# Three-term bfloat16 feed-forward with ternary weights in a four-layer gated block

## Chip, cores and metric

The kernel runs on one core of one Trainium2 chip. The metric is the device time of one execution in microseconds (us), as the median of several runs. Profile times come from one further execution under the hardware profiler, and count from the start of its span.

## What is computed

The reference is a stack of four layers, each a cross attention and a feed-forward. Both work on the layer-normalised activations `x` (4 x 256 tokens of 256 features, float32) and are added back through a gate `tanh(g)`. The layers differ in their attention and in their feed-forward: layer 0 a mixture of 16 experts, layer 1 a feed-forward with ternary weights, layer 2 a matmul quantised to 8 bits, layer 3 a mixture of 8 experts. Here layer 1's feed-forward is changed:

```python
def absmean_quant(w):
    scale = jnp.mean(jnp.abs(w))
    mask = (jnp.abs(w) >= scale * 0.7).astype(w.dtype)
    return jnp.sign(w) * mask                       # -1, 0 or 1
w1_q, w2_q = absmean_quant(w1), absmean_quant(w2)   # 1024 x 256, 256 x 1024
h = gelu(x @ w1_q.T + b1)                           # 1024 tokens x 1024
out = h @ w2_q.T + b2                               # 1024 tokens x 256
```

## The kernel before

`x` stays in on-chip memory (SBUF) for the whole kernel as eight tiles of 128 tokens by 256 features. Most work goes by two groups `g` of 512 tokens (`NG` = 2, four tiles each)[...]. The eight steps (attention and feed-forward of each layer) are written one after the other. The program is written as a dataflow on tiles: a scheduler sets the order of instructions on each engine ahead of the run and adds the waits on semaphores, so each engine runs its own fixed list. A tile of a pool tag has as many buffers as the tag's `bufs`: `mm` in PSUM has four banks, `t4` in SBUF six buffers of 1024 float32 columns, `xn` six, `xT` two.

Names that matter here:

- `big` is one large SBUF tensor of 24,576 float32 columns. It holds layer 0's attention weights and experts first. Then its second part serves as `latents()` (from column 16,384 on, the hidden values of attention 1 and of layer 1's feed-forward), and at last it holds layer 3's eight experts, 3,072 columns each.
- `load_experts3` (L297) issues two DMAs for each expert of layer 3 on the SP queue. Experts 0 to 4 are loaded at the end of `ffn0`, experts 5 to 7 after `ffn1`, when `hidden` has been read. SP's queue is in order; the loads of the shared expert (`L3_sgu`, `L3_sd`) stand in it too.
- `ternary1` (L1425) is a generator whose steps are spread over layer 0's expert loop. It makes the ternary weights of layer 1 in place on VectorE (L1451, L1452), as float32.
- `ffn1` (L1455) is the step that is changed. `normalised` makes the layernorm on VectorE (L372), transposes it on TensorE (L384) and evacuates PSUM to `xT` by ScalarE and VectorE in turn (L129, L131). `up` does 8 x 2 matmuls of 128 x 128 weights by 512 tokens for a group (L399, in the helper `mm2`), and ScalarE writes `gelu` to `hidden` (L1468). `down` does 8 matmuls for each 128 tokens, with `hidden` as the stationary side and 256 columns of `w2` moving (L1475). VectorE adds the bias into `y` (L1479) and then adds to `x` (L434). `in_turn` orders this as up of group 0, up of group 1, down of group 0, down of group 1.

Lines that the text names in other stages: L656 and L664 are products and sums of attention 0's rotary embedding on VectorE and on POOL (GpSimd), L406, L407 and L415 the steps of a softmax on VectorE, ScalarE and POOL, L838 and L1047 two 16-bit matmuls, L1490 and L1491 roundings of layer 2's quantisation on VectorE.

Of the kernel before, what the change touches and what calls it, by code (L numbers as in the profile page):

```python
# [34 lines left out]
ALU = mybir.AluOpType  # L35
# [35 lines left out]
BIG = E3 * W3  # L71
X0W = E0 * W0
HALF = 16384
NOWHERE = 16384.0
C_SLOTS = 3

# [2 lines left out]
def tile_flamingo(ctx: ExitStack, tc: tile.TileContext, a: dict, out: bass.AP):  # L79
# [7 lines left out]
    def ps_mm():  # L87
        return psum.tile([P, 512], F32, tag="mm", name="mm", bufs=4)
# [299 lines left out]
    def normalised():  # L388

        out = []  # L390
        for g in range(NG):
            xn = layernorm(g)
            out.append((transposed(xn), xn))
        return out

    def mm2(ps, w, xT):

        for c in range(2):
            nc.tensor.matmul(ps, w(c), xT[:, c, :], start=(c == 0), stop=(c == 1))  # L399
# [180 lines left out]
    def latents():  # L580
        t = big[:, HALF:].rearrange("p (g r t) -> p g r t", g=NG, r=NP)
        return [t[:, g] for g in range(NG)]
# [678 lines left out]
    def ffn0(gate):  # L1261
        normal = normalised()
        xT = [xt for xt, _ in normal]
        xd = stored([xn for _, xn in normal], "xd0")
        work, places = big[:, X0W : BIG - 400], Carver(big[:, BIG - 400 :])
        cut = Carver(work)
        route: list = []

        def routing():
            cw, mask = yield from chosen(xT, gate0, E0, K0, gate0_b, gate, 2, cut)  # L1270
            route.append(cw)
            route.append((yield from placed(cw, mask, E0, K0, NB0, W0, cut, places)))

        steps = routing()
        next(steps)
        s13 = loaded["L0_s13"][:, : 2 * W0U].rearrange("p (j c n) -> p j c n", j=2, c=2)
        s2 = loaded["L0_s2"][:FC0, :1024].rearrange("p (j f o) -> p j f o", j=2, f=2)
        held: dict = {}

        def up(t):  # L1280
            g, i = divmod(t, TPG)
            ps = ps_wide()
            for j in range(2):
                nc.tensor.matmul(
                    ps[:, j, : 2 * F0], shared_is[:, j : j + 1].to_broadcast([96, P]), bias_0, start=True, stop=False
                )
            for c in range(2):
                for j in range(2):
                    nc.tensor.matmul(
                        ps[:, j, : 2 * F0], xT[g][:, c, i * P : (i + 1) * P], s13[:, j, c, :], start=False, stop=(c == 1)  # L1290
                    )
            st = t4([P, 1024], "shared")
            s = st[:, : 2 * F0].rearrange("p (j f) -> p j f", j=2)
            nc.scalar.activation(s, ps[:, :, :F0], AF.Silu)
            nc.vector.tensor_tensor(s, ps[:, :, F0 : 2 * F0], s, ALU.mult)
            held[t] = st
            next(steps, None)

        def turn(t):
            ps = ps_mm()  # L1300
            for j in range(4):
                nc.tensor.transpose(ps[:FC0, j * P : (j + 1) * P], held[t][:, j * FC0 : (j + 1) * FC0], ident)
            nc.scalar.copy(held[t][:FC0, 512:], ps[:FC0])
            next(steps, None)

        def down(t):
            hT = held.pop(t)[:FC0, 512:]
            ps = ps_mm()
            for j in range(4):
                nc.tensor.matmul(  # L1310
                    ps[:, :D], hT[:, j * P : (j + 1) * P], s2[:, j // 2, j % 2, :], start=(j == 0), stop=(j == 3)
                )
            gated_add(t, ps[:, :D], gate)

        in_three(NT, up, turn, down)
        for _ in steps:
            pass
        used("L0_s13")
        used("L0_s2")
        cw, placing = route  # L1320
        expert = placing[2]
        choice = places([96, NB0], BF16)
        nc.vector.tensor_scalar(choice, expert[:96], expert_of, None, ALU.is_equal)

        def hTs(st, b):
            return st[:FC0, 432:688]

        diags = work[:, : PEK * NT * P].rearrange("p (k t c) -> p k t c", k=PEK, t=NT)
        fold = fold1()
        ended = []  # L1330
        ternary = ternary1()

        def between(i):
            if i % 4 == 3 and not ended:
                try:
                    next(fold)
                except StopIteration as end:
                    ended.append(end.value)
            if i > 40 and ended:
                next(ternary, None)  # L1340
            if 8 <= i < 8 + PEK * NT:
                k, t = divmod(i - 8, NT)
                nc.vector.tensor_scalar(diags[:, k, t, :], ident, placing[4][:, k, t : t + 1], None, ALU.mult)

        moe = Experts(placing, xd, K0, NB0, W0, F0, FC0, "z0", big[:, : E0 * W0], (bias_0, choice), hTs, between)
        moe.run()
        kept["fold1"] = ended[0]
        for t in range(NT):

            def bias(ps):  # L1350
                pt = ps_mm()
                nc.tensor.transpose(pt[:X0, :P], cw[:, t, :], ident)
                cwT = sb.tile([P, D], F32, tag="xn", name="cwT", bufs=6)[:X0, :P]
                nc.scalar.copy(cwT, pt[:X0, :P])
                nc.tensor.matmul(ps, cwT, b2_0, start=True, stop=False)
                return True

            done = moe.combine(t, 3, {k: diags[:, k, t, :] for k in range(PEK)}, bias)
        load_experts3(0, 5, done)
        for _ in ternary:  # L1360
            pass

# [59 lines left out]
            moe.combine(t, K3, {})  # L1422

    def ternary1():  # L1425

        n = D * 1024
        sums = small([P, 2], "sums", 1)
        for k in range(2):
            part = small([P, 16], "part", 2)  # L1430
            for i in range(4):
                nc.vector.tensor_reduce(
                    part[:, i * 4 : (i + 1) * 4],
                    loaded[f"L1_w{k + 1}"][:, i * 512 : (i + 1) * 512].rearrange("p (a b) -> p a b", a=4),
                    AX.X,
                    ALU.add,
                    apply_absolute_value=True,
                )
                yield
            nc.vector.tensor_reduce(sums[:, k : k + 1], part, AX.X, ALU.add)  # L1440
        ps = ps_mm()
        nc.tensor.matmul(ps[:, :2], ones, sums, start=True, stop=True)
        thr = small([P, 2], "thr", 1)
        nthr = small([P, 2], "nthr", 1)
        nc.vector.tensor_scalar(thr, ps[:, :2], 1.0 / n, 0.7, ALU.mult, ALU.mult)
        nc.vector.tensor_scalar(nthr, thr, -1.0, None, ALU.mult)
        for k in range(2):
            for i in range(4):
                v = loaded[f"L1_w{k + 1}"][:, i * 512 : (i + 1) * 512]
                low = sb.tile([P, 512], F32, tag="low", name="low", bufs=1)  # L1450
                nc.vector.tensor_scalar(low, v, nthr[:, k : k + 1], None, ALU.is_le)  # L1451
                nc.vector.scalar_tensor_tensor(v, v, thr[:, k : k + 1], low, ALU.is_ge, ALU.subtract)  # L1452
                yield

    def ffn1(gate):  # L1455
        b2_1 = output_bias("b2_1", a["L1_b2"].partition_broadcast(P))
        quant = [loaded["L1_w1"], loaded["L1_w2"]]
        w1 = quant[0].rearrange("p (c f) -> p c f", c=2)
        w2 = quant[1].rearrange("p (f o) -> p f o", f=8)
        xT = [x for x, _ in normalised()]  # L1460
        hidden = latents()

        def up(g):
            h = hidden[g]
            for f in range(8):
                ps = ps_mm()
                mm2(ps, lambda c: w1[:, c, f * P : (f + 1) * P], xT[g])
                nc.scalar.activation(h[:, f, :], ps, AF.Gelu, bias=b1_1[:, f : f + 1])  # L1468
            return h

        def down(g, h):
            for i in range(TPG):
                ps = ps_mm()
                for f in range(8):
                    nc.tensor.matmul(  # L1475
                        ps[:, :D], h[:, f, i * P : (i + 1) * P], w2[:, f, :], start=(f == 0), stop=(f == 7)
                    )
                y = sb.tile([P, D], F32, tag="xn", name="y", bufs=6)
                nc.vector.tensor_tensor(y, ps[:, :D], b2_1, ALU.add)  # L1479
                gated_add(g * TPG + i, y, gate)  # L1480

        in_turn(NG, up, down)
        used("L1_w1")
        used("L1_w2")
        load_experts3(5, E3)

    def quantised(q, v, inv):
# [177 lines left out]
```

## Time and profile before

| what | value |
|---|---|
| median of 3 runs | 1029.69 us (1029.3 to 1032.34) |
| the profiled execution | 1034.87 us, its span 1033.2 us |
| TensorE (PE) busy | 922.9 us, 89% |
| VectorE (DVE) busy | 511.2 us, 49% |
| ScalarE (ACT) busy | 276.0 us, 27% |
| GpSimd (POOL) busy | 308.9 us, 30% |
| mean granted TensorE clock | 0.948 |

The step `ffn1` lies between 603.9 and 666.0 us. Busy times are sums over the whole span. A float32 matmul is two records in the profile, each with a weight load (PEld) of its own. The end of a matmul is modelled, so its duration has a fixed part, and the distance between starts is the better measure of a stream. Engines work side by side. What one of them costs is read from the stage and from the chain of waits, not from its share.

### The profile page before, as it was taken

The numbers are of one execution on the slowest core, as the hardware profiler recorded it, in microseconds if no ns is written. First come the engines' busy times: TensorE is split into PE (matmuls) and PEld (weight loads), VectorE is DVE, ScalarE is ACT, GpSimd is POOL, SyncE is SP. The second block draws the span as 40 slices with busy tenths as digits, with TensorE's granted clock in tenths as the row PEclk, the third lists the DMA queues.
The fourth block names the chain that finished last, engine by engine and source line by source line (L and its number), as shares of the span: only waits on it lengthen the run. The fifth ranks groups of instructions, "written<-read, shape, count | busy, mean of one in ns | idle before, by whom it ended". The sixth has DMA issues, their size and how long they took to land.

```text
span 1033.2 us, 12983 instructions
## 1 busy us (share of the span) xinstructions
PE 922.9 (89%) x4527; PEld 604.8 (59%) x4527; DVE 511.2 (49%) x1202; ACT 276.0 (27%) x544; POOL 308.9 (30%) x298
## 2 busy tenths in 40 slices
PE   3999998999799999998899989979658899999993
PEld 3544435876668876675547855745334556566661
DVE  6535446757833334453627720568676772212223
ACT  2111113442123233232123433035204431222220
POOL 4345442210256666572002210014002302233311
PEclk9999999999989999998999999989668999999997
DMA  9200118000234333532850000510000001111103
GB/s 325 82 15 0 31 46 280 21 29 3 75 115 166 115 112 124 158 77 90 272 194 1 1 1 25 185 45 1 21 0 1 22 21 30 35 47 41 32 16 123
DMA packets 36350, 76.99 MB, mean 75 GB/s; under 512 B 5434, under 2 KB 22640, under 8 KB 34975
## 3 DMA queue, kind: packets, MB, share of 16 engines
q1 hardware_dynamic: 27551, 55.88, 16.0%
q0 software_dynamic: 8736, 20.28, 6.7%
q8 instruction: 39, 0.64, 0.3%
q14 instruction: 24, 0.20, 0.1%
HBM read 64.59 MB, written 14.42 MB: 76 GB/s over the span
## 4 chain that ended last, share of the span: by engine, by line
PE 59%; DVE 16%; issue 13%; DMA 4%; POOL 4%; ACT 3%; SPq 0%; POOLq 0%; DVEq 0%; ACTq 0%
PE wide L399 8%; PE wide L1151 6%; PE mm L1186 5%; PE mm L630 4%; PE mm L399 4%; PE mm L1475 3%; PE wide L1385 2%; PE mm L429 2%; PE wide L1162 2%; POOL zz L1198 2%; PE mm L1177 2%; PE mm L890 1%; PE mm L691 1%; PE mm L384 1%; PE mm L1134 1%
## 5 line engine op out<-in xcount | busy, mean ns | idle before, releaser
L415 POOL TENSOR_TENSOR attn<-attn,sm 128x1024 f32<-128x1024 f32 x32 | 60.8, 1901 | 227.1 <-DVE sm L414 156.9
L1171 DVE TENSOR_TENSOR blk<-wide,blk 128x176 f32<-128x176 f32 (+1 forms) x86 | 37.3, 434 | 169.3 <-ACT blk L1170 169.3
L656 DVE TENSOR_TENSOR rope<-wide,big 128x512 f32<-128x512 f32 x96 | 59.6, 682 | 65.3 <-PE wide L399 65.3
L1151 PE MATMUL wide<-big,blk 128*128 x252 | 87.3, 469 | 0.3 <-issue 0.3
L399 PE MATMUL wide<-xT,big 128*128 128x512 f32 x192 | 87.3, 601 | 0.0
L1122 POOL DMA_INDIRECT xs<-xd,big x63 | 62.6, 993 | 79.1 <-PE mm L1177 36.6
L1162 PE MATMUL wide<-big,blk 128*128 x184 | 83.0, 593 | 0.5 <-DVE blk L1136 0.5
L1198 POOL DMA_INDIRECT zz<-ring,big x63 | 64.5, 1024 | 33.8 <-DVE ring L1195 14.0
L1170 ACT ACTIVATE blk<-wide 128x176 f32<-128x176 f32 (+1 forms) x86 | 33.7, 392 | 143.7 <-PE wide L1151 71.4
L1186 PE MATMUL mm<-big,blk 88*128 x252 | 65.0, 379 | 0.5 <-ACT blk L1179 0.5
L399 PEld LDWEIGHTS wide<-xT,big 128*128 128x128 f32 x192 | 35.0, 190 | 48.1 <-issue 38.3
L630 PE MATMUL mm<-vo,attnT 128*128 128x256 f32 x256 | 61.1, 393 | 0.9 <-ACT attnT L430 0.9
L1186 PEld LDWEIGHTS mm<-big,blk 88*128 88x128 f32 x252 | 47.5, 189 | 17.7 <-ACT blk L1179 1.4
L1151 PEld LDWEIGHTS wide<-big,blk 128*128 128x128 f32 x252 | 46.3, 194 | 16.0 <-issue 2.3
L630 PEld LDWEIGHTS mm<-vo,attnT 128*128 128x128 f32 x256 | 49.1, 197 | 9.7 <-ACT attnT L430 3.3
L430 ACT COPY attnT<-mm 128x512 f32<-128x512 f32 x64 | 35.0, 588 | 67.8 <-PE mm L429 67.8
L1162 PEld LDWEIGHTS wide<-big,blk 128*128 128x128 f32 x184 | 33.1, 190 | 33.2 <-issue 32.5
L1136 DVE COPY blk<-mm 128x256 f32<-128x256 f32 x86 | 36.0, 419 | 31.8 <-PE mm L1134 31.8
L1122 POOL DMA_INDIRECT xs<-xd,scratch x23 | 22.2, 966 | 92.5 <-PE mm L1134 71.3
L384 PE MATMUL mm<-ident,xn 128*128 128x128 f32 x128 | 26.1, 346 | 25.6 <-DVE xn L372 13.0
L429 PE MATMUL mm<-ident,attn 128*128 128x128 f32 x256 | 37.6, 295 | 11.8 <-POOL attn L415 11.8
L413 DVE TENSOR_REDUCE sm<-attn 128x16 f32<-128x1024 f32 x32 | 38.9, 1214 | 14.6 <-ACT attn L407 12.5
(346 smaller groups left out, 1690.0 us busy)
## 6 DMA issues: line engine op xcount, KB each, us to landing
big<-in_L_w_gate_up SPq DMA_DIRECT2D x8, 1024.0 KB, 10.1
zt<-zz SPq DMA_DIRECT2D x16, 384.0 KB, 4.7
big<-in_L_w SPq DMA_DIRECT2D x4, 1408.0 KB, 6.8
big<-in_L_w_down SPq DMA_DIRECT2D x8, 512.0 KB, 8.7
w_L_qk<-in_L_qk SPq DMA_DIRECT2D x4, 896.0 KB, 15.2
big<-in_L_w SPq DMA_DIRECT2D x4, 704.0 KB
big<-in_L_wo SPq DMA_DIRECT2D x1, 2048.0 KB, 19.7
xd<-xn SPq DMA_DIRECT2D x16, 128.0 KB, 1.8
```

The costliest lines, as they stand in the source:

```text
L399: nc.tensor.matmul(ps, w(c), xT[:, c, :], start=(c == 0), stop=(c == 1))
L413: nc.vector.tensor_reduce(sm, e, AX.X, ALU.add)
L415: nc.gpsimd.tensor_tensor(e, e, sm.unsqueeze(2).to_broadcast([P, groups, n]), ALU.mult)
L429: nc.tensor.transpose(ps[:, i * P : (i + 1) * P], ev[:, pr * P : (pr + 1) * P], ident)
L630: nc.tensor.matmul(ps[:, :D], aT[:, s, :], vo[:, s, :], start=(s == 0), stop=(s == NP - 1))
L656: nc.vector.tensor_tensor(m[:, s, :].rearrange("q (b t) -> q b t", t=S), ps[:, s, :].rearrange("q (b t) -> q b t", t=S), table, ALU.mult,)
L1122: nc.gpsimd.indirect_dma_start(out=xs, out_offset=None, in_=self.xd, in_offset=bass.IndirectOffsetOnAxis(ap=self.gather[:, b : b + 1].bitc ...
L1151: nc.tensor.matmul(ps[:, 0, : 2 * n], st[:, c * P : (c + 1) * P], self.w[:, bass.ds(r + c * 2 * n, 2 * n)], start=False, stop=(c == 1),)
L1162: nc.tensor.matmul(ps[:, k, :n], st[:, c * P : (c + 1) * P], self.w[:, bass.ds(r + (2 * c + k) * n, n)], start=(c == 0), stop=(c == 1),)
L1171: nc.vector.tensor_tensor(s, lin, s, ALU.mult)
L1186: nc.tensor.matmul(ps[:, :D], hT[:, j * P : (j + 1) * P], self.w[: self.chunk, bass.ds(r + j * D, D)], start=(j == 0), stop=(j == self.n - 1),
L1198: s = nc.gpsimd.indirect_dma_start(out=self.z, out_offset=bass.IndirectOffsetOnAxis(ap=self.scatter[:, b : b + 1].bitcast(U32), axis=0), i ...
```

## The change

The activations of layer 1's feed-forward are split into three bfloat16 terms: the value rounded to bfloat16, the rounded rest, and the rounded rest of that. Each term is multiplied by the ternary weights, which bfloat16 holds exactly, and the three products are summed in PSUM. So a float32 matmul becomes three bfloat16 matmuls, each with a weight load.

- `ternary1` writes its result as bfloat16 into the first half of the weights' own buffer.
- `inputs(g)` takes the place of `normalised`: for each half of the features ScalarE copies PSUM to the first term, VectorE subtracts it from PSUM, ScalarE copies the rest to the second term, and VectorE subtracts that into the third. The third terms lie in a `t4` buffer, `more`.
- `up` writes `gelu` for two `f` (1024 columns) into a `t4` buffer `h`. `three_terms` splits it: ScalarE copies the first term, POOL subtracts it from `h` in place, VectorE copies the second term, and VectorE subtracts to the third. The terms of all `f` lie in `big` from column 12,288 on (`HIDDEN`), which is the place of experts 4 to 7.
- `down` uses three terms for each `f`, 24 matmuls for each 128 tokens.
- Experts 0 to 3 of layer 3 are now loaded at the end of `ffn0`, and experts 4 to 7 after `ffn1`.

```diff
+EARLY3 = 4
+HIDDEN = EARLY3 * W3
...
-        load_experts3(0, 5, done)
+        load_experts3(0, EARLY3, done)
...
+    def ternary(k):
+        return loaded[f"L1_w{k}"][:, :1024].bitcast(BF16)
+
+    def three_terms(terms, v, rest):
+        nc.scalar.copy(terms[0], v)
+        nc.gpsimd.tensor_tensor(rest, v, terms[0], ALU.subtract)
+        nc.vector.tensor_copy(terms[1], rest)
+        nc.vector.tensor_tensor(terms[2], rest, terms[1], ALU.subtract)
...
-                nc.vector.scalar_tensor_tensor(v, v, thr[:, k : k + 1], low, ALU.is_ge, ALU.subtract)
+                nc.vector.scalar_tensor_tensor(
+                    ternary(k + 1)[:, i * 512 : (i + 1) * 512], v, thr[:, k : k + 1], low, ALU.is_ge, ALU.subtract
+                )
...
-        quant = [loaded["L1_w1"], loaded["L1_w2"]]
-        w1 = quant[0].rearrange("p (c f) -> p c f", c=2)
-        w2 = quant[1].rearrange("p (f o) -> p f o", f=8)
-        xT = [x for x, _ in normalised()]
-        hidden = latents()
+        w1 = ternary(1).rearrange("p (c f) -> p c f", c=2)
+        w2 = ternary(2).rearrange("p (f o) -> p f o", f=8)
+        hidden = big[:, HIDDEN:].bitcast(BF16).rearrange("p (g k f t) -> p g k f t", g=NG, k=3, f=8)
+
+        def inputs(g):
+            two = sb.tile([P, 2, 2, TH], BF16, tag="xT", name="xT", bufs=2)
+            more = t4([P, 1024], "more")
+            third = more[:, :512].bitcast(BF16).rearrange("p (c t) -> p c t", c=2)
+            xn = layernorm(g)
+            for c in range(2):
+                ps = ps_mm()
+                for i, n in enumerate(xn):
+                    nc.tensor.transpose(ps[:, i * P : (i + 1) * P], n[:, c * P : (c + 1) * P], ident)
+                rest = more[:, 512:]
+                nc.scalar.copy(two[:, 0, c, :], ps)
+                nc.vector.tensor_tensor(rest, ps, two[:, 0, c, :], ALU.subtract)
+                nc.scalar.copy(two[:, 1, c, :], rest)
+                nc.vector.tensor_tensor(third[:, c, :], rest, two[:, 1, c, :], ALU.subtract)
+            return two[:, 0], two[:, 1], third
+
+        xT = [inputs(g) for g in range(NG)]
 
         def up(g):
-            h = hidden[g]
-            for f in range(8):
-                ps = ps_mm()
-                mm2(ps, lambda c: w1[:, c, f * P : (f + 1) * P], xT[g])
-                nc.scalar.activation(h[:, f, :], ps, AF.Gelu, bias=b1_1[:, f : f + 1])
-            return h
-
-        def down(g, h):
+            for f2 in range(4):
+                h = t4([P, 2, TH], "h")
+                for j in range(2):
+                    f = 2 * f2 + j
+                    ps = ps_mm()
+                    for k, term in enumerate(xT[g]):
+                        for c in range(2):
+                            nc.tensor.matmul(
+                                ps,
+                                w1[:, c, f * P : (f + 1) * P],
+                                term[:, c, :],
+                                start=(k == 0 and c == 0),
+                                stop=(k == 2 and c == 1),
+                            )
+                    nc.scalar.activation(h[:, j, :], ps, AF.Gelu, bias=b1_1[:, f : f + 1])
+                three_terms([hidden[:, g, k, 2 * f2 : 2 * f2 + 2, :] for k in range(3)], h, h)
+            return hidden[:, g]
+
+        def down(g, terms):
             for i in range(TPG):
                 ps = ps_mm()
                 for f in range(8):
-                    nc.tensor.matmul(
-                        ps[:, :D], h[:, f, i * P : (i + 1) * P], w2[:, f, :], start=(f == 0), stop=(f == 7)
-                    )
+                    for k in range(3):
+                        nc.tensor.matmul(
+                            ps[:, :D],
+                            terms[:, k, f, i * P : (i + 1) * P],
+                            w2[:, f, :],
+                            start=(f == 0 and k == 0),
+                            stop=(f == 7 and k == 2),
+                        )
...
-        load_experts3(5, E3)
+        load_experts3(EARLY3, E3)
```

## Prediction, made before the changed kernel was run

> **What bounds the kernel now.** I read the page's busy table first: TensorE 922.9 of 1033.2 us. That is an average, so I went to the stage that is edited, by the chain of waits (columns: start, length, what):
>
> ```profile
> 604.23 0.45 PE mm L384 x4
> ...
> 608.98 1.27 PE mm L384 x6
> 610.25 27.68 PE mm L399 x62
> 637.93 27.64 PE mm L1475 x128
> 665.57 0.02 issue
> 665.59 0.42 DVE y L1479
> ```
>
> From the first transpose (604.2) to the last `y` (666.01) TensorE sets the time: 27.7 us up, 27.6 us down, nothing between. The busy time by stretch and the groups of the stage show how idle the others are (stretch: engine busy us, records; then group: busy, mean ns, idle before):
>
> ```profile
> 610.00:638.00 28.00, 28.00 (x66) 12.47 (x65) 0.69 (x1) 11.85 (x18) 0.00 (x0) 0.96 0.00 0
> 638.00:666.00 28.00, 28.00 (x130) 24.40 (x129) 11.22 (x31) 2.23 (x3) 0.00 (x0) 1.00 0.38 135
> ```
>
> ```profile
> L399 PE MATMUL mm<-xT,w_L_w 128*128 128x512 f32 x64 | 28.9, 611 | 0.0
> L1475 PE MATMUL mm<-w_L_w,big 128*128 128x256 f32 x128 | 27.8, 379 | 0.0
> L1468 ACT ACTIVATE big<-mm,b 128x512 f32<-128x512 f32 x16 | 11.0, 687 | 16.1 <-PE mm L399 16.1
> ```
>
> POOL has 0.00 us in both stretches, VectorE 11.9 of 56. A float32 matmul is two records: 64 records are 32 matmuls, 128 are 64. Pitch 27.64/128 = 0.216 us a record of 256 columns, twice that for 512.
>
> The prices of the new work are in other stages (the timeline for the first two lines, groups by shape for the others):
>
> ```profile
> 589.05 0.59 PE L838 MATMUL wide<-causal,ident 128*128 128x512 bf16 x2
> 270.67 0.62 PE L1047 MATMUL mm<-big 128*128 128x126 f16 x8
> ```
>
> ```profile
> L415 POOL TENSOR_TENSOR attn<-attn,sm 128x1024 f32<-128x1024 f32 x32 | 60.8, 1901 | 227.1 <-DVE sm L414 156.9 <-issue 49.0 <-PE mm L630 8.2
> L664 POOL TENSOR_TENSOR qr<-rope 128x512 f32<-128x512 f32 x12 | 15.3, 1273 | 35.1 <-DVE rope L656 35.1
> L406 DVE TENSOR_TENSOR attn<-wide,mx 128x1024 f32<-128x1024 f32 x16 | 19.5, 1217 | 0.2
> L407 ACT ACTIVATE attn<-attn 128x1024 f32<-128x1024 f32 x16 | 16.9, 1058 | 15.6 <-DVE attn L406 15.6
> ```
>
> Two bfloat16 matmuls of 512 columns take 0.59 and one alone 0.38, so the pitch is 0.21 us. Eight 16-bit pairs of weight load and 126-column matmul take 0.62, one 0.22: pitch 0.057, so at 256 columns (0.107) a separate weight load should not bind.
>
> **What the Trainium skill says.** "SBUF — State Buffer", section "SBUF: two separate sides": VectorE's second port pair is GpSimd's only one, an exclusive lock held for the whole instruction. It is taken by a VectorE operation in a two-port mode, or with two SBUF inputs against a GpSimd operation that reads SBUF. The trace is in line with it but does not prove it: of the 64 `L372` (SBUF to SBUF) none overlaps a POOL tensor operation, while of the 96 `L656` (one operand in PSUM) 55 do, at an unchanged 678 to 693 ns. Two SBUF inputs against POOL occur nowhere. "VectorE: DVE Perf Modes", "The perf-mode tier table": a float32 SBUF copy runs at 2x, `tensor_tensor` at 1x. The trace agrees: `L1451` (512 wide) takes 483 ns and the like `L1490` (256) 342, so 0.55 ns an element, and `L406` 1.19. "GPSIMD Engine Reference", section 3.1: a 2048-wide add takes 4497 ns; with `L664` at 1273 for 512 that gives 2.35 us for 1024 (an estimate). "TensorE: Matmul & The Clock Gate", Part 1: after some 3.4 us idle the clock halves until as long a busy stretch; the trace grants 0.52 in 740 to 760, where TensorE is busy 8.2 of 20 us.
>
> **The change part by part.**
>
> *Matmuls.* Up: 96 at 0.213 = 20.4 us against 27.7. Down: 192 at 0.11 (0.107 and a little) = 21.1 against 27.6. Gain if TensorE stays the bound: 7.3 + 6.5 = 13.8 us.
>
> *Inputs.* The four evacuations become eight ScalarE copies (0.59, half of them from SBUF) and eight VectorE subtractions (0.69). The layernorm of the second half must pass between them on VectorE, and TensorE works two `f` at once meanwhile. By adding the queues up from 604.5 on, the first half's third term is ready at 611.4 instead of a plain `xT` at 605.8; by 612.3 twelve of the 96 matmuls are done, where the stream before began at 610.25. Start lost: 612.3 - 12 x 0.213 = 609.7 against 610.25 - 2 x 0.43 = 609.4 before, 0.3 us. Then the first Gelu follows its table load (1.28) at 613.2.
>
> *ScalarE.* 16 Gelus at 0.60 (0.687 less the overlap of neighbours), 8 copies of 1024 (1.06 by `L407`) at 1.0, two late input copies: 18.6 us from 613.2, so about 632, against 630.2 for the matmuls. Close to balance: 1 to 2 us of the gain go here, in the first half only.
>
> *The split of `hidden`.* Eight blocks of 1024 columns, each in series: ScalarE copy, POOL subtraction (2.35), VectorE copy (0.285 of `L1491` at 256 + 768 x 0.55 ns = 0.71), VectorE subtraction (1.22 by `L406`). Side by side POOL needs 18.8 us, VectorE 15.4: hidden under 41 us of matmuls. But all three take the shared pair: the copy by its two-port mode, both subtractions by two SBUF inputs. Serial, a block costs 2.35 + 0.71 + 1.22 = 4.28, and with three handovers at some 0.07 (an estimate: the `L372` of 203.97 and 581.63 start 68 and 66 ns after a POOL end) **4.5 us; eight are 36 us**. I take the serial value; both ends stay in the range.
>
> *Where that lands.* First ScalarE copy done at 616.5 (three Gelus and a late input copy take 2.3 us from 613.2, then its own 1.06). Last block: 616.5 + 36 = 652.5. TensorE has finished up by 632; the four tiles of the first `down` have their blocks by 634.5, or up to 642 where POOL gets the pair first, and take 4 x 24 x 0.11 = 10.6 us. The second `down` cannot run ahead: `mm` has four banks, its first tile takes the bank of tile 0, and in the order in which the changed program is built VectorE's addition for tile 0 stands behind the last block's copy, so ends at 652.5 - 0.8 = 651.7. Then 10.6 us for four tiles, 0.9 for a cold start (0 if TensorE came late to the first four, 1.7 if it idled), 0.6 for drain and `y`: 663.8. **Against 666.0: 2.2 us gained.** In one formula the stage ends at 616.5 + 8b + 11.3, b the block's price; b = 4.78 is no gain.
>
> *Ternary weights.* Same eight `L1452`, written as bfloat16 in place: input still two float32 tensors, so 746 ns as before. Cover: the expert stage, where TensorE is busy 19.9 of 20 us in 440 to 460. Uncovered, a changed rate could cost or give 3 us in all.
>
> *Expert loads.* Expert 4 (1.5 MB) moves from between 507 and 540 to after the first `down`; both its DMAs on SP then wait for `hidden`'s last reader. The shared expert's load stands among them on SP and is read at 827; the experts are read from 881. At the 262 GB/s seen in 650 to 660, 6 MB are 23 us, so all is in by 690: nothing, with over 100 us of cover, and nobody waited for the early load. POOL's bias load for the next stage comes behind the eight subtractions, but waits for the last `y` as now (666.31).
>
> Sum: -2.2 us. The profiled execution reads 1034.87 us (span 1033.2, 1.67 around it), 5.2 above the median of the three runs shown, 1029.69; I carry the difference to the median: 1027.5. About 0.3%, 3.1 us, is what a measurement here can tell from no change.
>
> **Rivals.**
>
> 1. *The pair is not shared for these operations.* For: `L656` runs beside POOL untouched. Against: the page's wording, and `L372`. If only the two-port copy blocks, 2.35 + 0.71 a block keeps up with ScalarE's 2.2 to 3.1: the last block is done near 643, the end 643 + 10.6 + 0.8 = 654.4, a gain of 11.6. With no blocking TensorE bounds throughout: 632 less a little + 21.1 + 0.6 = 652.2, a gain of 13.8. So 1015.9 to 1018.1.
>
> 2. *Slower: the block passes 4.78 us.* Place: POOL's mixed subtraction, float32 less bfloat16, of which the trace has none. At 3.3 instead of 2.35 us b is 5.45 and the end 671.4: 5.4 us lost, 1035.1. It decides from 2.65 us on. For: `L664` is already a third slower per element than `L415`, whose second operand is broadcast. Against: the element count is the same, and half the bytes of one operand.
>
> 3. *The matmuls do not stream at 0.107.* If a weight load for every 256 columns costs 0.125, TensorE loses 2.9 us, 1.5 of it in the second `down` that sets the end: 1029.0. Against: pitch 0.057 at 126 columns.
>
> **How the numbers follow.** Serial blocks, the forecast: 0.62 (rival 3 inside it). Its own range: b from 4.3 (no handovers) to 5.0 (copy at 1x, 1.22) gives a gain of 3.8 to a loss of 1.8, and the cold start moves it by 0.9; so 1025.0 to 1032.4. Of this, 0.24 is a gain over 3.1, 0.35 within, 0.03 a loss. Rival 1: 0.22, all faster. Rival 2: 0.16, all slower or nearly (0.15; 0.01 within). Faster 0.46, same 0.36, slower 0.18. The range reaches from 1015.5, which takes in rival 1, to 1034.5, half of rival 2.
>
> **What would show it.** Right: VectorE's third-term subtractions and POOL's subtractions never overlap and alternate at 4.3 to 4.7 us a block; TensorE idles between about 632 and 651 for 7 to 9 us, ended by VectorE; the last four tiles run about 10.6 us; the stage ends at 662 to 665. Wrong: POOL and VectorE subtracting at once (rival 1); a POOL subtraction over 2.65 us (rival 2); a `down` tile over 2.9 us (rival 3); idle TensorE anywhere from 700 on that was not there before (then the moved loads count).

## The result, and the profile after

The changed kernel takes 1024.01 us (median of 20 runs, 1018.87 to 1027.71) against 1029.47 us for the kernel before (20 runs, 1024.58 to 1033.28) on the same chip. The ratio is **0.9942**, with a 95% interval of 0.9927 to 0.9957: about 6.0 us faster.

Below, "the stage" is the time from the end of the last matmul of attention 1 (L630 before, L632 after) to the end of the last `y`. It begins at 604.23 us before and at 600.69 us after. It took 61.8 us before (604.23 to 666.01) and takes **56.1 us** after (600.69 to 656.78), so 5.7 us were gained in it, which agrees with the runs (the interval is 4.4 to 7.5 us). The two profiled executions differ by more, 1034.87 to 1023.56 us: 3.5 us of that lie ahead of the stage and 2.1 behind it. Single runs of one kernel spread over nearly 9 us, so these parts say nothing. Times after a "+" count from the start of the stage, so that kernels can be compared.

The chain of waits of the changed kernel, in the stage (start, length, what):

```profile
614.56 2.26 DVE more L1490
616.82 2.58 DVE big L1435
...
619.43 3.03 DVE big L1436
622.46 2.55 DVE big L1435
...
625.04 1.22 DVE big L1436
...
634.44 1.24 DVE big L1436
635.67 0.05 issue
635.72 20.62 PE mm L1519 x172
656.34 0.02 issue
656.36 0.42 DVE y L1527
```

Before, this chain was TensorE alone. Now VectorE carries it from 614.56 to 635.67: the copy to the second term (L1435) and the subtraction to the third (L1436), block after block. Only then does TensorE run to the end, 172 of the 192 matmuls of `down` without a gap.

The same stretch as busy time by engine (stretch: length, then PE, PEld, DVE, ACT and POOL busy us with records, granted clock, DMA share, GB/s):

```profile
616.80:635.70 18.90, 14.29 (x73) 6.96 (x72) 18.76 (x10) 13.90 (x18) 17.67 (x7) 1.00 0.13 35
635.70:645.30 9.60, 9.58 (x73) 7.96 (x74) 9.49 (x10) 0.00 (x0) 1.94 (x1) 0.82 0.01 2
```

VectorE shows 18.8 of 18.9 us busy, and POOL 17.7. Both look full, but they are not at work at the same time. The groups by shape show it (busy, mean ns of one, idle before):

```profile
L1519 PE MATMUL mm<-w_L_w,big 128*128 128x256 bf16 x192 | 23.3, 285 | 4.5 <-DVE big L1436 2.7 <-DVE big L1435 1.8
L1434 POOL TENSOR_TENSOR h<-h,big 128x1024 f32<-128x1024 f32 x8 | 21.8, 2744 | 20.8 <-issue 19.1 <-DVE big L1435 1.2 <-ACT big L1433 0.4
L1435 DVE CAST big<-h 128x1024 bf16<-128x1024 f32 x8 | 15.2, 1896 | 0.0
L1436 DVE TENSOR_TENSOR big<-h,big 128x1024 bf16<-128x1024 f32 x8 | 13.4, 1676 | 0.2
```

A copy of 1024 columns averages 1896 ns here. It takes 0.69 us where POOL is quiet and 2.62 where it meets a POOL subtraction. In the same way L1436 takes 1.22 or 3.03, L1490 of the input 0.69 or 2.26, and POOL's L1434 takes 2.13 alone and up to 3.2. **The wait is recorded inside the duration**: no row shows idle time for it. Two lines of the timeline, of POOL and of VectorE, show one such case; the copy ends 0.55 us after the second POOL operation has ended at 618.84:

```profile
616.71 7.74 POOL L1434 TENSOR_TENSOR h<-h,big 128x1024 f32<-128x1024 f32 x3 [0.43 <-ACT big L1433]
616.75 2.65 DVE L1435 CAST big<-h 128x1024 bf16<-128x1024 f32 x1
```

And TensorE, by the timeline:

```profile
628.49 1.69 PE L1519 MATMUL mm<-w_L_w,big 128*128 128x256 bf16 x14
631.93 0.72 PE L1519 MATMUL mm<-w_L_w,big 128*128 128x256 bf16 x5 [1.74 <-DVE big L1436]
634.46 0.28 PE L1519 MATMUL mm<-w_L_w,big 128*128 128x256 bf16 x1 [1.81 <-DVE big L1435]
635.72 20.60 PE L1519 MATMUL mm<-w_L_w,big 128*128 128x256 bf16 x172 [0.98 <-DVE big L1436]
```

It ended `up` at +27.8 and began `down`, but tile 0 needs all four blocks of group 0. It stood still for 4.5 us, in three pieces, first for the third term of block 2 and then for the second and the third term of **block 3**, the last of group 0, which was there at 635.66 (+35.0). The first 16 of the 172 matmuls then ran at a pitch of 0.213 instead of 0.110, because the granted clock was 0.5 from 635.7 to 639.1: another 1.6 us.

POOL had by then done seven of its eight subtractions, three of them for group 1. Its timeline from block 4 on:

```profile
625.05 8.80 POOL L1434 TENSOR_TENSOR h<-h,big 128x1024 f32<-128x1024 f32 x3 [0.60 <-DVE big L1435]
634.46 3.18 POOL L1434 TENSOR_TENSOR h<-h,big 128x1024 f32<-128x1024 f32 x1 [0.60 <-DVE big L1435]
```

### The profile page after: what moved, and what is told of

Its sections match the earlier page's. It is cut to its first block, busy times and chain, and to the rows that moved or that the text cites. A ratio compares the mean times of both kernels' runs of the same rounds, so it can differ in the third digit from the quotient of the medians.

```text
span 1021.9 us, 13235 instructions
## 1 busy us (share of the span) xinstructions
PE 909.0 (89%) x4621; PEld 594.2 (58%) x4623; DVE 544.2 (53%) x1224; ACT 286.1 (28%) x558; POOL 330.8 (32%) x306
## 4 chain that ended last, share of the span: by engine, by line
PE 53%; DVE 18%; issue 16%; POOL 4%; DMA 4%; ACT 4%; SPq 1%; POOLq 0%; DVEq 0%; ACTq 0%
PE wide L401 8%; PE wide L1153 6%; PE mm L1188 5%; PE mm L632 4%; PE wide L1387 2%; POOL zz L1200 2%; PE mm L431 2%; PE mm L1519 2%; PE mm L401 2%; PE mm L693 1%; PE mm L892 1%; PE mm L679 1%; PE mm L1247 1%; PE mm L1179 1%; PE wide L617 1%
## 5 line engine op out<-in xcount | busy, mean ns | idle before, releaser
L658 DVE TENSOR_TENSOR rope<-wide,big 128x512 f32<-128x512 f32 x96 | 59.6, 683 | 65.3 <-PE wide L401 65.3
L1200 POOL DMA_INDIRECT zz<-ring,big x63 | 64.6, 1025 | 33.7 <-DVE ring L1197 13.9
L1172 ACT ACTIVATE blk<-wide 128x176 f32<-128x176 f32 (+1 forms) x86 | 33.7, 392 | 141.8 <-PE wide L1153 68.9
L632 PE MATMUL mm<-vo,attnT 128*128 128x256 f32 x256 | 60.5, 390 | 1.0 <-ACT attnT L432 0.9
L1188 PEld LDWEIGHTS mm<-big,blk 88*128 88x128 f32 x252 | 47.5, 189 | 17.7 <-ACT blk L1181 1.4
L1153 PEld LDWEIGHTS wide<-big,blk 128*128 128x128 f32 x252 | 46.0, 193 | 15.9 <-issue 2.0
L632 PEld LDWEIGHTS mm<-vo,attnT 128*128 128x128 f32 x256 | 48.4, 194 | 9.8 <-ACT attnT L432 3.5
L386 PE MATMUL mm<-ident,xn 128*128 128x128 f32 x112 | 23.4, 352 | 23.7 <-DVE xn L1540 12.3
```

The source lines that it names most:

```text
L632: nc.tensor.matmul(ps[:, :D], aT[:, s, :], vo[:, s, :], start=(s == 0), stop=(s == NP - 1))
L658: nc.vector.tensor_tensor(m[:, s, :].rearrange("q (b t) -> q b t", t=S), ps[:, s, :].rearrange("q (b t) -> q b t", t=S), table, ALU.mult,)
L1153: nc.tensor.matmul(ps[:, 0, : 2 * n], st[:, c * P : (c + 1) * P], self.w[:, bass.ds(r + c * 2 * n, 2 * n)], start=False, stop=(c == 1),)
L1188: nc.tensor.matmul(ps[:, :D], hT[:, j * P : (j + 1) * P], self.w[: self.chunk, bass.ds(r + j * D, D)], start=(j == 0), stop=(j == self.n - 1),
L1200: s = nc.gpsimd.indirect_dma_start(out=self.z, out_offset=bass.IndirectOffsetOnAxis(ap=self.scatter[:, b : b + 1].bitcast(U32), axis=0), i ...
```

## The experiments

Two theories stood against each other at first. **Exclusion**: a VectorE operation of the split and a POOL subtraction cannot run at once, so a block is the sum of its three operations. **No exclusion**: the long records come from traffic or from the chain of handovers. Each experiment is a change to the changed kernel, except e4. This table sums up the profiled executions; ratios are to the kernel before on the same chip, with their 95% intervals (e4 and e6 to e8 ran on another chip than e1, e2, e3 and e5). "Third term" is the one that held TensorE in `down`; in e3 and e7, where none did, it is that of block 3.

| kernel | stage us | third term at | ratio |
|---|---|---|---|
| before | 61.8 | | 1 |
| after | 56.1 | +35.0 | 0.9942 (0.9927 to 0.9957) |
| e1_dve_rest | 49.2 | no wait | 0.9864 (0.9827 to 0.9901) |
| e2_dve_rest_pool_idle | 65.1 | +43.9 | 1.0027 (1.0012 to 1.0041) |
| e3_act_second | 57.0 | +30.8, no wait | 0.9952 (0.9931 to 0.9973) |
| e4_loads_only | 61.8 | | 1.0005 (0.9979 to 1.0030) |
| e5_dve_rest_two_rests | 49.3 | no wait | 0.9853 (0.9825 to 0.9881) |
| e6_pool_group1 | 56.2 | +35.4 | 0.9956 (0.9935 to 0.9977) |
| e7_pool_group0 | 52.6 | +30.4, no wait | 0.9894 (0.9850 to 0.9937) |
| e8_dve_rest_pool_fill | 50.7 | +31.2 | 0.9895 (0.9845 to 0.9945) |

Among the changes to the changed kernel, only e1, e2 and e5 have an interval clear of its own. The others are told from it by their stages, and a stage is one profiled execution. The stages are not alike from the start, either: between +8.1 and +9.9 the granted clock was 0.50 in e2, e7 and e8, and 1.00 in the changed kernel, e1, e3 and e6. The first Gelu came at +11.1 in the three and at +9.9 to +10.1 in the four. This 1.1 us lies ahead of the first operation of the stage that the edits of e2, e7 and e8 touch, and has to be taken off when their stages are compared.

### e1_dve_rest: VectorE does all three steps

```diff
-        nc.gpsimd.tensor_tensor(rest, v, terms[0], ALU.subtract)
+        nc.vector.tensor_tensor(rest, v, terms[0], ALU.subtract)
```

> The subtraction of the first term moves from POOL to VectorE, so POOL does nothing in the stage. Theory (VectorE and POOL exclude each other for all three operations of a block): the block costs 1.22 + 0.69 + 1.22 = 3.1 us on VectorE alone instead of the 3.9 measured; block 3's third term is ready at about 614 + 4 x 3.1 = 626.5, before up ends at 628.7, and TensorE bounds the rest: the stage ends at 628.7 + 192 x 0.11 + 0.6 = 650.4 instead of 656.8, 6.4 us faster than the changed kernel, about 12.4 faster than the kernel before (ratio 0.988). Rival (no exclusion; the long durations have another cause, such as traffic in SBUF): VectorE now has 3.1 us a block to itself where POOL's 2.13 ran beside VectorE's 1.9, so the change brings nothing or loses: ratio 0.994 or above.

The groups of this kernel in the stage, and the end of its chain:

```profile
L1519 PE MATMUL mm<-w_L_w,big 128*128 128x256 bf16 x192 | 21.1, 273 | 0.0
L1434 DVE TENSOR_TENSOR h<-h,big 128x1024 f32<-128x1024 f32 x8 | 9.5, 1217 | 0.7 <-ACT big L1433 0.7
L1436 DVE TENSOR_TENSOR big<-h,big 128x1024 bf16<-128x1024 f32 x8 | 9.5, 1215 | 0.0
L1435 DVE CAST big<-h 128x1024 bf16<-128x1024 f32 x8 | 5.2, 682 | 0.0
```

```profile
631.76 20.97 PE mm L1519 x192
```

VectorE does more work than before this edit and is done sooner: 24.2 us for all three groups, where two of them were recorded at 28.6. All 192 matmuls of `down` follow `up` without a wait. The stage is 49.2 us, 6.9 less than the changed kernel's (6.4 were expected), and the interval of its ratio lies wholly below that of the changed kernel. The rival, which expected no gain or a loss from giving VectorE more work, falls. This run alone does not show that exclusion is the reason: POOL, slower, is out of the chain as well.

### e2_dve_rest_pool_idle: the same, with a POOL subtraction that nobody waits for

`busy` is a buffer of its own; its subtraction is added work.

```diff
-        nc.gpsimd.tensor_tensor(rest, v, terms[0], ALU.subtract)
+        nc.gpsimd.tensor_tensor(busy, busy, terms[0], ALU.subtract)
+        nc.vector.tensor_tensor(rest, v, terms[0], ALU.subtract)
```

> As e1_dve_rest, and besides POOL makes one subtraction of the same size and types for each block into a buffer of its own that nobody reads. Theory (exclusion): a block costs POOL's 2.0 plus VectorE's 3.1, about 5.1 us; block 3 is ready at about 634.5, the last at 655, and the stage ends near 655 + 10.6 + 0.6 = 666: 9 to 16 us slower than e1_dve_rest, about the time of the kernel before (ratio 0.996 to 1.003); VectorE's subtractions are recorded at up to 3 us where POOL is at work. Rival (no exclusion): nobody waits for POOL, so the time is that of e1_dve_rest within 1 us and VectorE's durations stay at 0.69 and 1.22.

The stage goes from 49.2 to 65.1 us. Of these 15.9 us, 1.1 lie ahead of the first Gelu. From the end of block 0's ScalarE copy to block 3's third term VectorE takes 29.5 us instead of 14.2 for the same operations: 15.3 us for eight POOL operations whose results nobody reads, 1.9 us for each. The ratio to before is 1.0027, slower than the kernel before. The timelines of POOL and VectorE at the first block:

```profile
614.62 2.13 POOL L1437 TENSOR_TENSOR busy<-busy,big 128x1024 f32<-128x1024 f32 x1 [20.15 <-ACT big L1436]
614.64 3.19 DVE L1438 TENSOR_TENSOR h<-h,big 128x1024 f32<-128x1024 f32 x1 [0.68 <-ACT big L1436]
```

Both are released by the same ScalarE copy. POOL is 0.02 us ahead and finishes at 616.75 in its usual 2.13. VectorE's subtraction ends at 617.83, 1.08 us later. No data passes between them, and POOL is not slowed, as it would be if both only shared some traffic: VectorE waited while POOL was at work. This is **exclusion, shown**; whether any work of POOL has this effect is left to e8. It agrees with what the Trainium skill says on the page "SBUF — State Buffer", section "SBUF: two separate sides": the shared port pair belongs to one of the two for a whole instruction.

### e8_dve_rest_pool_fill: POOL as busy, but without reading

As e1, and POOL fills `busy` twice for each block, each fill bound to the block's ScalarE copy. The fills are added work.

```diff
-        nc.scalar.copy(terms[0], v)
-        nc.gpsimd.tensor_tensor(rest, v, terms[0], ALU.subtract)
+        made = nc.scalar.copy(terms[0], v)
+        for _ in range(2):
+            filled = nc.gpsimd.memset(busy, 0.0)
+            # filled waits for made
+        nc.vector.tensor_tensor(rest, v, terms[0], ALU.subtract)
```

> As e1_dve_rest, and besides POOL fills a buffer that nobody reads, twice 1024 columns a block (about 1.9 us), beginning with the ScalarE copy of the block: the same occupation of POOL as in e2_dve_rest_pool_idle, but without reading SBUF. Theory 1 (VectorE's two-input subtractions exclude POOL only when POOL reads, the two-port copy excludes it always): subtractions stay at 1.22 beside POOL, copies are recorded at up to 1.6 us, the block costs up to 4.0 us and the stage is 1 to 6 us longer than that of e1_dve_rest. Theory 2 (any work of POOL excludes any of the three): as e2_dve_rest_pool_idle, 12 us or more longer than e1_dve_rest. Theory 3 (a fill takes no port from VectorE): all durations as in e1_dve_rest and the same time.

The groups in the stage (L1445 and L1447 are the two subtractions, L1446 is the copy), and the first fills and the first subtraction by the timelines:

```profile
L1438 POOL MEMSET busy<- 128x1024 f32 x16 | 16.9, 1059 | 21.7 <-ACT big L1436 20.9
L1445 DVE TENSOR_TENSOR h<-h,big 128x1024 f32<-128x1024 f32 x8 | 9.5, 1215 | 0.7 <-ACT big L1436 0.7
L1447 DVE TENSOR_TENSOR big<-h,big 128x1024 bf16<-128x1024 f32 x8 | 9.5, 1213 | 0.0
L1446 DVE CAST big<-h 128x1024 bf16<-128x1024 f32 x8 | 7.9, 1018 | 0.0
```

```profile
622.69 1.96 POOL L1438 MEMSET busy<- 128x1024 f32 x2 [20.14 <-ACT big L1436]
622.74 1.23 DVE L1445 TENSOR_TENSOR h<-h,big 128x1024 f32<-128x1024 f32 x1 [0.68 <-ACT big L1436]
```

Theory 1 holds. The subtractions keep 1.21 us although they run beside fills; the first of them is at 622.74 to 623.97 and a fill at 622.69 to 623.64, both at their undisturbed length. The copy alone is longer, 1018 ns on average against 682 and up to 1.52 us, and fills that met a copy took 1.38 us instead of 0.95. The stage is 1.6 us longer than that of e1, at the low end of what was expected, but 1.1 of it lie ahead of the first Gelu and so of the first fill. From block 0's ScalarE copy to block 3's third term VectorE takes 16.8 us instead of 14.2; most of that is hidden behind `up`, and TensorE waits only 0.25 us for it. So it is the durations, more than the stage, that decide here, and they agree with the same page in its two finer points too: the copy, in its two-port mode, excluded both kinds of POOL work that were tried, and the subtractions with two SBUF inputs excluded only the kind that reads.

### e3_act_second: the copy on ScalarE

```diff
-        nc.vector.tensor_copy(terms[1], rest)
+        nc.scalar.copy(terms[1], rest)
```

> The copy to the second term moves from VectorE to ScalarE; POOL's and VectorE's subtractions stay. Theory (all three operations exclude each other): the pair is taken for 2.0 + 1.1 = 3.1 us a block instead of 3.9, ScalarE needs 2 x 0.6 + 2 x 1.05 = 3.3; block 3 is ready at 627 to 629, close to the end of up, and the kernel is 4 to 6 us faster than the changed one (ratio 0.988 to 0.990). Rival (only the copy in its two-port mode excludes POOL): with the copy gone POOL (2.13) and VectorE (1.22) run side by side at their undisturbed durations, their records overlap, and only ScalarE's 3.3 a block is left: also about 0.989, so it is the records of POOL and VectorE, overlapping or not, that tell the two apart.

This missed: no gain but 0.9 us lost against the changed kernel in the stage, and a ratio of 0.9952, which the runs do not tell from the changed kernel's. The two subtractions still exclude each other: POOL is recorded at 2.22 us and ends 1.99 us after VectorE's L1436, which it waits for at each block. The pair is no longer the bound, as expected; block 3 is ready at +30.8. But a group of this kernel shows what came in its place:

```profile
L1435 ACT CAST big<-h 128x1024 bf16<-128x1024 f32 x8 | 8.4, 1046 | 10.5 <-POOL h L1434 10.5
```

On ScalarE the copy stands ahead of the next Gelus, in an engine that works in order, and it waits 10.5 us in all for POOL. The Gelus behind it come late, the `mm` banks (in PSUM, where TensorE sums its products) stay full, and `up` ends at +33.7 instead of +27.8. The expectation counted ScalarE's work and not what is queued behind a wait. VectorE's timeline shows one more victim, far from the edit:

```profile
639.94 1.90 DVE L436 SCALAR_TENSOR_TENSOR x<-y,tg,x 128x256 f32<-128x256 f32 x1
```

L436 adds `y` to `x`, 256 columns from two SBUF inputs, and takes 0.48 us elsewhere. Here it met a POOL subtraction that ended at 641.56.

### e7_pool_group0 and e6_pool_group1: which wait ends last

The first subtraction is on POOL for one group of tokens and on VectorE for the other.

```diff
-        nc.gpsimd.tensor_tensor(rest, v, terms[0], ALU.subtract)
+        (first or nc.gpsimd).tensor_tensor(rest, v, terms[0], ALU.subtract)
...
+                three_terms(..., h, h, nc.vector if g else nc.gpsimd)   # e7; in e6 the other way round
```

> The reverse: POOL for group 0, VectorE for group 1. Theory A (POOL runs ahead: in the changed kernel it takes the pair for blocks of group 1 before block 3 has its third term, so the first four blocks cost 5.4 us each and the last four 2.4): without that, block 3 is ready at about 614 + 4 x 3.9 = 630 instead of 635.7, and the stage ends near 652, 4 to 5 us faster than the changed kernel. Theory B (block 3 is late for the price of its own four blocks): it is ready at 635 as before, and the stage is that of the changed kernel, 56 us, within 1 us. Rival (only the sum over eight blocks counts): 3.2 us faster, like e6_pool_group1.

> The first term's subtraction on VectorE for the four blocks of group 0 and on POOL for the four of group 1. Theory (a block is 3.1 us on VectorE alone and 3.9 shared; what starts the down stream is block 3): block 3 is ready at about 614 + 4 x 3.1 = 626.5, or up to 2 us later if POOL gets the pair for group 1 in between, so TensorE is held little or not; the last block is ready at about 642, and the end is 642 + 8.6 + 0.6 = 651 to 653: 4 to 6 us faster than the changed kernel (stage of 50 to 52 us against 56.1). Rival (only the sum over eight blocks counts): 4 x 0.8 = 3.2 us faster than the changed kernel, as e7_pool_group0.

**e7**: theory A holds. Block 3 is ready at +30.4 instead of +35.0, although its group is still split by POOL. In the changed kernel seven POOL subtractions were done by then, three of them for group 1, and three times 1.99 is 6.0 us. Measured from the first Gelu, which came 1.1 us later in e7's stage, block 3 gained 5.7. TensorE never waited for a third term, but its timeline shows another wait:

```profile
636.87 10.64 PE L1521 MATMUL mm<-w_L_w,big 128*128 128x256 bf16 x96
649.48 10.64 PE L1521 MATMUL mm<-w_L_w,big 128*128 128x256 bf16 x96 [1.97 <-DVE y L1529]
```

The second `down` stood 1.97 us for the `mm` bank of tile 0. Its `y` was done at 649.43, since VectorE had it in its list behind block 7's copy (648.41 to 649.09). The stage was 52.6 us where 51.3 were expected; this wait and the late first Gelu are more than the difference. By its size alone, 3.5 us against the changed kernel, the gain would fit the rival's 3.2 as well; it is block 3's time, and the comparison with e6, that speak for theory A.

**e6** missed: its stage is 56.2, no better than the changed kernel. POOL's and TensorE's timelines:

```profile
632.93 11.04 POOL L1434 TENSOR_TENSOR h<-h,big 128x1024 f32<-128x1024 f32 x4 [27.83 <-ACT big L1433]
646.25 20.25 PE L1521 MATMUL mm<-w_L_w,big 128*128 128x256 bf16 x172 [3.91 <-DVE big L1436]
```

TensorE waited for a third term until 646.20, +35.4. VectorE's list has block 4 (group 1, first step on POOL) ahead of block 3 in its last two steps. VectorE idled 2.02 us for POOL at 634.84 to 636.86, and then each of POOL's next two subtractions held up one of its copies, to 2.60 and 2.61 us. So the group that needs POOL delays the group that does not, once the scheduler lets the two interleave. That only the sum over eight blocks counts is excluded by the pair: e6 and e7 have the same sum, and their stages differ by 3.6 us, although e7's has the late first Gelu.

### e5_dve_rest_two_rests: a second buffer in the input split

As e1, with in `inputs`:

```diff
+            spare = t4([P, 2, TH], "spare")
...
-                rest = more[:, 512:]
+                rest = spare[:, c, :]
```

> As e1_dve_rest, and besides the two feature halves of the input split keep their rests in two buffers instead of one, so that the second half's subtraction need not wait for the first half's third term. Theory: with the block at 3.1 us TensorE bounds the stage, so an earlier start of up is worth what it moves: 0.5 to 1.5 us more than e1_dve_rest. Rival (the start of up is set by the layernorm of the second group on VectorE or by TensorE's transposes): the same as e1_dve_rest within 0.3 us.

The same: stage 49.3 against 49.2, `up` ends at +27.7 against +27.6, and the intervals of the two ratios overlap almost wholly. The third terms of the first group were ready at +5.3 instead of +7.0, and `up` was not done sooner. So the wait for the shared buffer was not what bound it; what did was not settled. e1 and e5 are the fastest versions that were run; their intervals (0.9825 to 0.9901 together) lie below that of the changed kernel.

### e4_loads_only: the kernel before with the late load

```diff
-        load_experts3(0, 5, done)
+        load_experts3(0, 4, done)
...
-                nc.vector.tensor_tensor(y, ps[:, :D], b2_1, ALU.add)
+                last[g] = nc.vector.tensor_tensor(y, ps[:, :D], b2_1, ALU.add)
...
-        load_experts3(5, E3)
+        load_experts3(4, 5, last[0])
+        load_experts3(5, E3)
```

> The kernel before with nothing changed but the loads of layer 3's experts: expert 4's two DMAs no longer stand at the end of ffn0 but follow the last y of the first down group, and experts 5 to 7 follow them. Theory (as predicted: over 100 us of cover): the same time as before within 0.3%, ratio 0.997 to 1.003. Rival (a load that is late or that collides holds part of the difference between the two kernels): faster or slower by 1 us or more outside the interval.

No difference: ratio 1.0005, and the stage is 61.78 us to the hundredth. The load did move: DMA carries 288 GB/s from 660 to 680, where it carried 164 before. So the moved loads are worth nothing, within the 0.3% of the interval.

## Why the prediction was right, and where it was off

Faster was the likeliest of the three outcomes, and the mechanism named for the forecast case, a split that is serial between POOL and VectorE and takes the place of TensorE as the bound, is what e2, e8 and the traces show. The outcome was in part luck. Of the 0.46 for faster, 0.22 belonged to rival 1, which e2 refutes; without it "same", with 0.36, would have been the likeliest. The gain was 2.2 us by the sum and 6.0 by the runs, a little beyond the forecast case's own range, which ended at 3.8 with 0.9 more for the cold start. In the terms of the sum, all from the start of the stage:

| term | predicted | measured |
|---|---|---|
| first ScalarE copy of a block done | +12.3 | +13.3 |
| from there to the last third term (8b) | 36.0 | 31.2 |
| from there to the end | 11.3 | 11.5 |
| stage | 59.6 | 56.1 |

- **The block's price was the mis-sized term**: 4.5 predicted, 31.2 / 8 = 3.9 measured. It was too high in three ways. POOL's subtraction, mixed operands and all, takes 2.13 us instead of the 2.35 estimated from the 4497 ns for 2048 columns in the Trainium skill's "GPSIMD Engine Reference", section 3.1, and from the trace. The handovers, 0.21 a block, did not show. And an operation that waits for the pair has its start-up behind it: after the other engine's end POOL needs 1.99 us, the copy 0.55 and the subtraction 1.08, each 0.14 less than alone. These three sum to 3.6; the rest of the 3.9 is the last input subtraction (L1490), tile 0's `y` and the operations that did not wait. The pair is what is scarce, and only the time in which it is held counts.
- **The blocks are not equal, and the gate was another one.** The forecast had POOL and VectorE take turns block by block, and the end gated by tile 0's `y` behind the last block's copy. In fact they mostly took turns operation by operation. VectorE needs two turns for a block and POOL one, so POOL ran ahead: seven of its eight operations were done when block 3 got its third term, and the first four blocks took 21.6 us and the last four 9.6. TensorE was released by block 3 and had work from then to the end; tile 0's `y` began at 643.70 while TensorE was still busy with the first `down`. That the tail term fits (11.3 and 11.5) is an accident. Tile 0's `y` was a true gate, but one that this kernel does not reach: e7 waits for it, 1.97 us.
- *Signs that failed with this*: TensorE's idle time was 4.5 us between 630.2 and 635.7, not 7 to 9 between 632 and 651. The operations did not alternate at 4.3 to 4.7 us a block. The stage ended at +56.1, not at +58 to +61. And "never overlap" cannot be read from the records: L1436's from 619.43 to 622.46 overlaps POOL's from 618.87 to 621.38, which looks like rival 1, because the wait lies inside the record. The ends tell: L1436's comes 1.08 us after POOL's.
- *Matmuls*: right. `down` in e1 runs 192 in 21.1 us, as predicted, and `up` has a pitch of 0.216 instead of 0.213. Rival 3 is out. The cold start, put at 0.9 with 1.7 as an end, was 1.6: the same 172 matmuls take 20.6 us in the changed kernel and 19.0 in e8, where TensorE waited only 0.25 us before them.
- *Inputs*: too low. The first Gelu starts at +10.0 instead of +9.0, and `up`, counted back from its end, starts 1.0 us later than before (27.8 - 96 x 0.216 = 7.1, against 33.5 - 64 x 0.429 = 6.1) instead of 0.3. In the changed kernel the late first Gelu is the 1.0 us in the first row of the table. In e1, where TensorE is the bound, the late start of `up` is most of why the stage gains 12.6 us instead of 13.8.
- *ScalarE*: its own work did not bind, but it was held by VectorE, since the buffers `h` come free with the third term: L1510 waited 4.8 us for L1436. The prediction had not named that wait. It costs little here: `up` ends at +27.8, and at +27.6 in e1, where nothing waits for it.
- *Ternary weights and loads at nothing*: right, the loads within what e4 can tell (0.3%). The eight operations of L1465 take 746 ns as before.
- *Rivals*: rival 1 (no sharing) is refuted by e2; its time, 1015.9 to 1018.1, is about what e1 reaches by taking POOL out (1017.73). Rival 2 needed a POOL subtraction over 2.65 us. The profile's mean of 2744 ns for L1434 looks like it, and is not it: it includes waits, and alone the operation takes 2.13.

Not settled: what decides who gets the pair when both want it. In the changed kernel a waiting operation nearly always got it at the next end, but in e6 VectorE kept it through two operations in a row; no run was made for it.

## What to carry to other kernels

Before work is moved to a free POOL, ask whether the VectorE operations beside it read two SBUF tensors or copy from SBUF; if so the durations add up, as they did here, and one engine doing all of it can be faster, as here by 6.9 us. Read a VectorE or POOL row whose mean is well above the same shape elsewhere as a wait, and price a shared resource by the time in which it is held. When blocks feed a consumer in groups, look for who takes the resource for a later group before the first one is complete.

## What the hardware showed that was not expected

- Waiting for the shared pair leaves no gap in the trace: a copy of 0.69 us was recorded at 2.62, and VectorE and POOL were 99% and 93% busy in the same stretch.
- The start-up of a blocked operation is hidden: each ran 0.14 us shorter from its release than alone (POOL 1.99 for 2.13, the copy 0.55 for 0.69, the subtraction 1.08 for 1.22).
- A fill by POOL left two-input subtractions at 1.21 us and pushed copies from 0.69 to as much as 1.52; a copy pushed a fill from 0.95 to 1.38.
- The pair need not change hands at the end of an operation: in e6 a POOL subtraction that was recorded from 632.93 waited through the ends of two VectorE operations (633.70 and 634.84), and ended 1.99 us after the second.
